# The last four row groups as one pair and two singles, with seven work tiles, five gate tiles, three cell tiles and two attention tiles

## The chip, the cores and the metric

The kernel runs on one core of a Trainium2 chip. The metric is the device time of one execution in microseconds (us), median of a few runs. A profiled execution has a span, which runs from its first to its last instruction, and a time of its own that lies a little above the span.

The engines go by the profile's names: PE is TensorE (PEld its weight loads), DVE is VectorE, ACT is ScalarE, POOL is GpSimd, and SP is SyncE, whose queue issues the transfers of the last phase.

## The reference

`x` has 128 batches of 64 nodes with 256 features, that is 8192 rows, and `adj` is a 64 x 64 matrix. Four graph layers follow one another, each as `x = layernorm(x + layer(x))`, all in float32:

- Layer 0 multiplies three times by `adj * adj` along the nodes and by a weight along the features (256 to 512 to 1024 to 256), with a ReLU after the first two.
- Layer 1 takes the eigenvectors `U` of a normalised Laplacian of `adj`, applies `U.T`, two small weights with a ReLU between, and `U`.
- Layer 2 applies `adj` and a weight twice, each with a ReLU, and then four LSTMs. For p = 1, 2, 3, 4, windows of p successive nodes are fed to LSTM p, and its last hidden state is written back at the last node of the window:

```python
for p in range(1, MAX_SKIP + 1):
    nw = Tv // p
    wins = h[:, :nw * p, :].reshape(Bv * nw, p, Hd)
    last = _lstm_last(Wih[p - 1], Whh[p - 1], bih[p - 1], bhh[p - 1], wins)
    idx = jnp.arange(nw) * p + (p - 1)
    h = h.at[:, idx, :].set(last.reshape(Bv, nw, Hd))
```

- Layer 3 is an attention within a batch: `h = x @ W + b_lin`, scores `h h^T` masked by `adj`, softmax, times `h`, plus `b`.

## The kernel before

The 8192 rows lie as 64 tiles of 128 rows, in 16 groups of 4 tiles, numbered 0 to 15. The first phase (to about 860 us of the span) does layer 0 for all groups and the eigenvectors in between. The second phase does layers 1, 2 and 3 for one group after another, and the change lies there alone.

In the second phase nothing is issued at once. Helpers (`Noted`, line 235; `products`, `turns`) write every operation into a `Plan` (line 104) with an assumed cost, the buffers that it reads and writes, and its predecessors. `Plan.run` (line 158) then picks the operations one by one, engine by engine, by the earliest time at which inputs, engine and a free buffer are there by its own clock, and emits them in that order. So the order of each engine's instructions is fixed when the program is built. As one helper emits everything, nearly all instructions of this phase carry line 156 in the profile, and one tells them apart by their tiles.

A **unit** is what `Plan.run` takes up at a time, with `UNITS = 3` units going side by side. Line 1554 makes the units: groups go in pairs up to `16 - SINGLE`, and the rest one by one.

```python
units = [(g, g + 1) for g in range(0, NT // 4 - SINGLE, 2)] + [(g,) for g in range(NT // 4 - SINGLE, NT // 4)]
plan.run([left_over] + [lambda u=u: unit(u) for u in units], UNITS)
```

`unit` (line 1518) does for each of its groups `layer1`, then `to_lstm` (the two products with `adj` and the LSTMs of p = 1, 2, 3), then the LSTM of p = 4, then `from_lstm` (the state transposed back, added to the rows, normalised) and `layer3`. A pair and a single group differ only in the LSTM of p = 4:

```python
if len(groups) == 2:
    four(hTs)
else:
    lstm(hTs[0], 4, 0, 16)
```

- `lstm` (line 1378) makes each gate of a step from four matmuls of 128 x 128 weights (two for the input, two for the hidden state) that stream 128 columns (16 windows of 8 batches). The first step has three gates and no hidden state. A gate goes from PSUM (tile `ps`) through a tanh on ACT into a tile `gates`; DVE then makes the cell `c` and the hidden state `hs`.
- `four` (line 1502) takes the first step the same way for each group. For the steps 1 to 3 it calls `halves` (line 1439), which treats the two groups and the two halves of the weights as a 2 x 2 block product and does it with seven products in place of eight. For that, DVE makes four differences or sums of the states (in a tile `w`), and seven more additions for each half `h` put the gates together. The sums of the weights (`sums`) are made once.

The last groups, `ENDING = (14, 15)`, do `layer3` in two parts of two tiles, and their row normalisations end on ACT (`norm`, line 1232, with `scalar`): statistics on DVE, four small operations on POOL (`rs`, `nm`), and then ACT applies them to `X`. After that SP stores the tile. In the other groups DVE applies them.

Buffers are slots of a tag: `w` (4 KB in each partition, `WIDE` of them; transposed rows, LSTM states, attention inputs), `gates` (4 KB, `GATES`), `c` (2 KB, `CELLS`), `hs` (`OUTS`), `att` (2 KB, `ATT`, cleared once by POOL), `v`, and the eight banks `ps`. A guard in `candidates` (line 168) lets a unit that is not the oldest take a slot only if enough stay free for the oldest (`MOST`, line 112: 4 of `w`, 2 of `gates`, 1 of `c` and of `att`).

When no unit is left to begin and at most `LASTS` groups have work left, the guard is dropped, and `rank` (line 163) lets PE take the group with the most operations left first.

Of the kernel before, what the change touches and what calls it, by code (L numbers as in the profile page):

```python
# [103 lines left out]
class Plan:  # L104
# [53 lines left out]
    def run(self, units, ways):  # L158
# [4 lines left out]
        def rank(op):  # L163
            if op.engine == "PE" and not todo and len(left) <= LASTS:
                return -left[op.group]
            return op.group or 99

        def candidates(guard):
            oldest = min([u for u in going if u] or [0])
            best = None  # L170
            for e, ops in able.items():
                first = []
                for op in ops:
                    t = max(self.free[e], op.ready)
                    for tile in op.tiles:
                        if tile.real is None and tile.slot is None:
                            s = self.slots[tile.tag]
                            t = max(t, min(s))

                            if (guard and op.unit != oldest and  # L180
                                    sum(x < 1e9 for x in s) <= self.MOST.get(tile.tag, 1) - held.get((oldest, tile.tag), 0)):
                                t = 1e9
                    if t < 1e9:
                        first.append((t, op))
                if first:
                    t0 = min(t for t, _ in first)
                    t, op = min((x for x in first if x[0] <= t0 + 0.02), key=lambda x: (rank(x[1]), x[1].rank))
                    if best is None or t < best[0]:
                        best = t, op
            return best  # L190

        while todo or going:
            while todo and len(going) < ways + (0 in going):
# [4 lines left out]
                for op in self.ops:  # L198
                    left[op.group] = left.get(op.group, 0) + 1
                    if not op.left:  # L200
                        able[op.engine].append(op)
            t, op = (candidates(True) if todo or len(left) > LASTS else None) or candidates(False)
            e = op.engine
# [535 lines left out]
EPS = 1e-5  # L739
UNITS = 3  # L740
ENDING = (14, 15)
WIDE = 6
GATES = 6
ATT = 3
CELLS = 4
OUTS = 4
LASTS = 3
SINGLE = 4

RING = 6  # L750

# [56 lines left out]
def kernel(  # L808
# [337 lines left out]
    att = []  # L1146
    for i in range(ATT):
        att.append(wb.tile([P, 4, P], F32, name=f"att{i}"))
# [3 lines left out]
    def place(tag, slot, shape):  # L1152
# [4 lines left out]
        if tag in ("w", "v", "gates", "c", "hs"):  # L1157
# [3 lines left out]
    plan = Plan({"PE": nc.tensor, "DVE": nc.vector, "ACT": nc.scalar, "POOL": nc.gpsimd, "SP": nc.sync}, place,  # L1161
                {"ps": 8, "w": WIDE, "v": 4, "gates": GATES, "c": CELLS, "hs": OUTS, "att": ATT, "mx": 4, "sm": 4, "st": 4, "mv": 4,
                 "rs": 4, "nm": 4})
# [354 lines left out]
    def unit(groups):  # L1518

        if groups[0] == 0:  # L1520
            add_weights(2, 30.0)
            add_weights(4, 60.0)
        xs, hTs = [], []
        for g in groups:
            plan.group = g + 1
            x = plan.tile("rows", [P, 4, D], rows_of(g % RING))
            xs.append(x)
            layer1(x)
            hTs.append(to_lstm(x))
        plan.group = groups[0] + 1  # L1530
# [4 lines that stand above are left out]
        for g, x, hT in zip(groups, xs, hTs):  # L1535
            plan.group = g + 1
            from_lstm(x, hT, g)
            if g in ENDING:
                layer3(x, g, 0, 2)
                layer3(x, g, 2, 2)  # L1540
            else:
                layer3(x, g, 0, 4)
            if g + RING < NT // 4:
                Q.dma_start(x, rest[g])
# [7 lines left out]
    with tc.manual_schedule(engines={mybir.EngineType.PE, mybir.EngineType.DVE, mybir.EngineType.Activation,  # L1552
                                     mybir.EngineType.Pool}):
        units = [(g, g + 1) for g in range(0, NT // 4 - SINGLE, 2)] + [(g,) for g in range(NT // 4 - SINGLE, NT // 4)]
        plan.run([left_over] + [lambda u=u: unit(u) for u in units], UNITS)
# [42 lines left out]
```

## Time and profile before

| | |
|---|---|
| median of 3 runs | 2471.87 us (2471.45 to 2472.79) |
| the profiled execution, its own time | 2474.36 us |
| its span | 2472.6 us |
| granted clock of PE, mean | 0.996 |
| busy in the span: PE / PEld / DVE / ACT / POOL | 99% / 87% / 65% / 43% / 6% |
| second phase, from about 860 us: PE / DVE busy | 1583 us / 963 us of 1612 us |
| transfers | 42.69 MB, most of it in the first slice |

The first block of the page gives each engine's busy time, the second the same in 40 equal slices of about 62 us, in tenths. A matmul in float32 appears as two records; a transpose appears as one. Matmuls are pipelined, so the duration of a record is longer than the distance to the next one; the distance is what a matmul costs when PE is full.

### The profile page before, as it was taken

The numbers are of one execution on the slowest core, as the hardware profiler recorded it, in microseconds if no ns is written. First come the engines' busy times: TensorE is split into PE (matmuls) and PEld (weight loads), VectorE is DVE, ScalarE is ACT, GpSimd is POOL, SyncE is SP. The second block draws the span as 40 slices with busy tenths as digits, with TensorE's granted clock in tenths as the row PEclk, the third lists the DMA queues.
The fourth block names the chain that finished last, engine by engine and source line by source line (L and its number), as shares of the span: only waits on it lengthen the run. The fifth ranks groups of instructions, "written<-read, shape, count | busy, mean of one in ns | idle before, by whom it ended". The sixth has DMA issues, their size and how long they took to land.

```text
span 2472.6 us, 40811 instructions
## 1 busy us (share of the span) xinstructions
PE 2438.2 (99%) x15500; PEld 2162.5 (87%) x15500; DVE 1618.9 (65%) x5676; ACT 1072.3 (43%) x2610; POOL 137.4 (6%) x316
## 2 busy tenths in 40 slices
PE   9999999999999999999999999999999999999997
PEld 7788888878887899989978999999998997988996
DVE  6888787778887274583674476476458468374336
ACT  2343343333333354444434444444444444445555
POOL 0000000000000010010010000000001001010002
PEclk9999999999999999999999999999999999999999
DMA  6000000000000110010000001001001000000000
GB/s 225 9 1 18 10 9 10 9 10 9 10 1 1 64 56 1 1 35 1 1 18 18 1 1 35 1 1 35 1 1 35 1 1 18 1 10 1 1 1 27
DMA packets 27973, 42.69 MB, mean 17 GB/s; under 512 B 2945, under 2 KB 22145, under 8 KB 27777
## 3 DMA queue, kind: packets, MB, share of 16 engines
q1 hardware_dynamic: 27424, 39.81, 4.6%
q8 instruction: 122, 2.00, 0.3%
q14 instruction: 75, 0.61, 0.1%
q10 hardware_dynamic: 352, 0.28, 0.0%
HBM read 26.45 MB, written 13.63 MB: 16 GB/s over the span
## 4 chain that ended last, share of the span: by engine, by line
PE 93%; DVE 5%; POOL 1%; DMA 1%; ACT 0%; issue 0%; SPq 0%; ACTq 0%; POOLq 0%; DVEq 0%
PE ps L156 61%; PE ps L940 31%; DVE X L156 1%; DVE D L52 1%; DVE st L156 1%; PE pc L296 1%; DMA XA<-in_x_dram 1%; DVE gates L156 0%; POOL rs L156 0%; DVE tw L52 0%; DVE w L156 0%; ACT gates L156 0%; DVE h L52 0%; DVE u L52 0%; DVE mv L156 0%
## 5 line engine op out<-in xcount | busy, mean ns | idle before, releaser
L156 PE MATMUL ps<-w,wih 128*128 128x168 f32 (+2 forms) x4144 | 753.7, 315 | 0.9 <-DVE gates L156 0.9
L156 PEld LDWEIGHTS ps<-w,wih 128*128 128x128 f32 x4144 | 647.6, 191 | 38.1 <-issue 6.9
L156 ACT ACTIVATE gates<-ps,cbi 128x168 f32<-128x168 f32 (+2 forms) x832 | 342.8, 418 | 368.5 <-PE ps L156 360.3
L156 PE MATMUL ps<-hs,whh 128*128 128x168 f32 (+1 forms) x1952 | 344.8, 291 | 0.0
L156 PEld LDWEIGHTS ps<-hs,whh 128*128 128x128 f32 x1952 | 289.2, 191 | 1.7 <-issue 1.4
L156 PE MATMUL ps<-w,sums 128*128 128x128 f32 x1776 | 237.1, 275 | 0.0
L156 DVE SCALAR_TENSOR_TENSOR gates<-gates 128x256 f32<-128x256 f32 (+2 forms) x220 | 84.0, 382 | 222.8 <-ACT gates L156 222.2
L940 PE MATMUL ps<-aw,h 128*128 128x256 f32 x1024 | 227.2, 379 | 0.0
L156 PEld LDWEIGHTS ps<-w,sums 128*128 128x128 f32 x1776 | 217.5, 192 | 0.6 <-issue 0.5
L940 PEld LDWEIGHTS ps<-aw,h 128*128 128x128 f32 x1024 | 192.9, 190 | 25.9 <-ACT h L949 0.5
L156 ACT ACTIVATE gates<-gates,cbi 128x256 f32<-128x256 f32 x272 | 116.4, 497 | 206.6 <-DVE gates L156 206.5
L949 ACT ACTIVATE h<-h 128x512 f32<-128x512 f32 x128 | 80.5, 630 | 196.6 <-DVE h L52 196.5
L156 DVE TENSOR_TENSOR gates<-gates,ps 128x256 f32<-128x256 f32 x340 | 128.7, 417 | 21.3 <-PE ps L156 15.9
L940 PE MATMUL ps<-ss,tw 128*128 128x256 f32 x512 | 117.9, 380 | 0.0
L940 PE MATMUL ps<-ss,aw 128*128 128x256 f32 x512 | 117.3, 379 | 0.0
L940 PE MATMUL ps<-m,aw 128*128 128x256 f32 x512 | 117.1, 380 | 0.0
L156 DVE SCALAR_TENSOR_TENSOR c<-gates,c 128x256 f32<-128x256 f32 (+2 forms) x156 | 57.2, 367 | 88.6 <-ACT gates L156 88.2
L940 PE MATMUL ps<-aw,m 128*128 128x512 f32 x256 | 114.8, 594 | 0.1
L940 PEld LDWEIGHTS ps<-ss,aw 128*128 128x128 f32 x512 | 96.6, 190 | 12.8
L940 PEld LDWEIGHTS ps<-ss,tw 128*128 128x128 f32 x512 | 96.3, 190 | 12.9 <-issue 0.2
L156 DVE TENSOR_TENSOR gates<-v,ps 128x256 f32<-128x256 f32 x136 | 55.5, 417 | 79.5 <-ACT v L156 47.7
L940 PEld LDWEIGHTS ps<-m,aw 128*128 128x128 f32 x512 | 95.6, 190 | 12.6 <-issue 0.5
(314 smaller groups left out, 3743.0 us busy)
## 6 DMA issues: line engine op xcount, KB each, us to landing
out_dram<-X SPq DMA_DIRECT2D x64, 128.0 KB, 1.7
rest<-XA SPq DMA_DIRECT2D x10, 512.0 KB, 2.6
X<-rest SPq DMA_DIRECT2D x10, 512.0 KB, 3.2
XA<-in_x_dram SPq DMA_DIRECT2D x18, 256.0 KB, 6.2
wih<-in_c_ih_dram SPq DMA_DIRECT2D x4, 1024.0 KB, 7.4
aw<-in_a_w_dram SPq DMA_DIRECT2D x3, 1024.0 KB, 10.8
X<-in_x_dram SPq DMA_DIRECT2D x12, 256.0 KB, 5.9
whh<-in_c_hh_dram SPq DMA_DIRECT2D x3, 1024.0 KB, 9.3
```

What stands on the lines that cost most here:

```text
L52: return getattr(self.engine, name)(out, *args, **kw)
L156: getattr(e, name)(*[real(x) for x in args], **{k: real(v) for k, v in kw.items()})
L296: PE.matmul(out, lhsT, rhs, start=True, stop=True)
L940: PE.matmul(out, lhsT, rhs, start=start, stop=stop)
L949: S.activation(dst, src, AF.Relu)
```

## The change

Six numbers at the head of the second phase are changed, and nothing else:

```diff
 ENDING = (14, 15)
-WIDE = 6
-GATES = 6
-ATT = 3
-CELLS = 4
+WIDE = 7
+GATES = 5
+ATT = 2
+CELLS = 3
 OUTS = 4
-LASTS = 3
-SINGLE = 4
+LASTS = 2
+SINGLE = 2
```

`SINGLE = 2` makes groups 12 and 13 a pair, so that seven pairs and two singles are left of six pairs and four singles. `LASTS = 2` applies the rule of the ending when two groups are left, not three. The four buffer counts give one tile of `w` (4 KB in a partition) for one of `gates` (4 KB), and free one of `c` and one of `att` (2 KB each). As all orders come from the plan, every engine's order in the second phase is a new one; the first phase keeps its order.

## The prediction

> **What bounds the kernel now.** I read the page's first two blocks, then tables of busy time by stretch, then the timeline of PE alone.
>
> ```profile
> span 2472.6 us, 40811 instructions
> PE 2438.2 (99%) x15500; PEld 2162.5 (87%) x15500; DVE 1618.9 (65%) x5676; ACT 1072.3 (43%) x2610; POOL 137.4 (6%) x316
> ```
>
> PE is the bound: 34.4 us of the span are without it. So a matmul less is worth its full price, and all else must come out of those 34.4 us. Where they lie is seen by stretch (columns: stretch, length, busy PE, PEld, DVE, ACT, POOL, then the clock granted to PE, DMA share, GB/s):
>
> ```profile
> 861.00:1250.00 389.00, 388.07 (x2800) 362.83 (x2799) 240.71 (x683) 184.33 (x450) 24.17 (x49) 1.00 0.05 20
> 1250.00:1320.00 70.00, 63.85 (x390) 50.40 (x389) 50.67 (x146) 29.35 (x59) 9.47 (x20) 0.95 0.09 31
> 1320.00:2030.00 710.00, 708.47 (x5167) 661.04 (x5166) 433.56 (x1274) 329.25 (x798) 35.55 (x72) 1.00 0.03 10
> 2030.00:2070.00 40.00, 36.36 (x273) 28.57 (x272) 32.59 (x94) 17.54 (x34) 5.85 (x12) 1.00 0.00 1
> 2070.00:2420.00 350.00, 349.63 (x2537) 330.50 (x2536) 168.47 (x504) 171.84 (x442) 12.36 (x24) 1.00 0.02 6
> 2420.00:2473.00 53.00, 36.87 (x286) 29.72 (x284) 36.74 (x125) 25.16 (x61) 15.07 (x40) 0.88 0.09 31
> ```
>
> PE idles 6.15 us at 1250 to 1320, 3.64 us at 2030 to 2070, 16.1 us in the tail from 2420, and 2.8 us in the other three together. In the two stretches in the middle DVE is 72% and 81% busy, against 60% around them; the finer table by 10 us has it at 9.4 to 9.9 of 10 at the worst places. The longest gap, on PE's timeline:
>
> ```profile
> 1302.32 1.29 PE L156 MATMUL ps<-adT,X 128*128 128x128 f32 x8 [3.64 <-DVE X L156]
> 1303.41 8.88 PE L156 MATMUL ps<-w,wih 128*128 128x256 f32 x33
> ```
>
> PE waited 3.64 us for DVE's normalised rows. After it, 33 records took 8.88 us; at the 0.2145 us of a full PE (two records of 256 columns 0.43 us apart near 2446) they would take 7.1. So the gap cost a further 1.8 us at a lower clock, and the two stretches cost 6.15 + 1.8 + 3.64 = 11.6 us.
>
> **What the Trainium skill says.** "TensorE: Matmul & The Clock Gate", section "What's actually happening", has the clock halved after an idle window of about 3.4 us, and restored after as much busy time. The trace agrees: the 3.64 us gap is followed by slow matmuls, while 2030 to 2070, whose longest gap is 2.05 us, stays at 1.00. "Perfetto Trace Analysis", section "Optimization Strategy", says to look for gaps on the bounding engine and what blocks it, and that a gap that repeats can mean too few buffers. Here the gaps do not repeat: two places hold most of them, behind a crowded DVE. I take that as a matter of order, which buffer counts decide only through the plan.
>
> **The change part by part.**
>
> *Groups 12 and 13 as a pair.* Two singles of p = 4 issue 2 x (3 gates x 2 halves x 2 + 3 steps x 4 x 2 x 4) = 2 x 108 = 216 matmuls of 128 columns. A pair issues 24 in its first step and 3 x 2 x 7 products x 4 = 168 after it: 192. So **24 fewer**, and the counts of the two built programs say the same (7976 and 7952 PE instructions, no other size touched). The price, from PE's timeline:
>
> ```profile
> 2405.26 0.61 PE L156 MATMUL ps<-hs,whh 128*128 128x128 f32 x4
> 2405.70 0.61 PE L156 MATMUL ps<-w,wih 128*128 128x128 f32 x4
> ...
> 2410.62 0.61 PE L156 MATMUL ps<-hs,whh 128*128 128x128 f32 x4
> ```
>
> From 2405.26 to 2410.62 there are 12 steps of two matmuls in 5.36 us, 0.2233 us each. 24 x 0.2233 = **5.4 us less**, all on the bound.
>
> *What it adds on DVE:* 42 additions of 256 columns (30 at 0.379, 12 at 0.408 us: 16.3), 24 differences of the states at 0.27 (6.6), 22 operations on `gates`, `c`, `hs` at 0.42 (9.3), less 44 of half the width at 0.29 (12.8): **+19.4 us**. ACT: 48 fewer tanh of one gate (0.352), 24 more of two (0.428), and small ones: -5.6 us. Both are hidden as long as DVE is not the last: DVE has about 60% in the phase. POOL clears one `att` less. SP's 142 transfers stay; none is moved past another that matters, as the rows of a group come in a whole unit ahead.
>
> *The order in the middle.* This is the unknown. The trace of before cannot show a new order, so I bound it: at best all 11.6 us of the two stretches go; at worst stalls of that kind grow (see rivals). To choose between, I laid DVE's instructions of the two built programs against PE's, in bins of 4 us of PE work, with durations from the trace, and carried DVE's surplus on. In the kernel before, the surplus is largest at 400 to 436 us of PE work (4.2 and 3.3 us, the place of the first stretch), at 1160 to 1192 (3.7, the second), and at 1012 (3.4, no gap of note). In the changed order no surplus is over 3.1 us, and only three are over 2.1; yet the densest 40 us still hold 40.1 us of DVE work, as before (40.4). So the crowding is spread rather than gone. I take half of the 11.6, rounded: **-5.5 us**. Fewer `gates`, `c` and `att` tiles I cost at nothing beyond this: waits for them show in no row of before, and the plan lays other groups' matmuls there.
>
> *The ending.* Take E as the end of the last LSTM matmul. Before, E is 2426.4 (2425.76 + 0.61), and 46.2 us follow, with 27.0 us of PE work in them (the third-last group's layer 3 is still to do): 19.3 us without PE. In the new order only the layer 3 of 14 and 15 is left, 19.1 us of PE work, and the transposes of both groups stand right behind E with nothing between. By durations of the trace: tanh 0.4, four copies on ACT (0.6 each) to E + 2.8; PE's transposes to 3.4; DVE's four sums (0.65) to 4.4, first statistics at 5.5; POOL 1.6 us for a normalisation, the next 1.67 later (2463.95 and 2465.62): 7.2, 8.9, 10.5, 12.2; ACT, which applies them between its copies, is through at 15.9; the last weight product follows at 18.7; 8.5 us of PE work and some 3.5 us of waits for exponentials put PE's end at 30.7; DVE 2.4, POOL two normalisations, ACT 1.1 and the store (2.6, from 2470.0 to the end) give E + 39.7. That is 20.5 us without PE, **+1.2 us**, give or take 3: what is late is POOL's chain and then ACT, which nothing covers any more.
>
> *Steps with two groups alone.* For 100 us before E only 14 and 15 remain. A step's first use of `hs` has at least 1.34 us of PE work between it and the last gate; before, the same places had 1.14 and 1.34, inside stretches with PE at 100%. Cost 0.
>
> Sum: -5.4 - 5.5 + 1.2 = **-9.7 us**. The execution that gave the durations took 2474.36 us, 1.8 more than its span and 2.5 more than the median of the runs; I take the difference from the median: 2471.87 - 9.7 = **2462.2 us**.
>
> **The rivals.**
>
> *Stalls stay as they are.* The crowded stretches only move. For it: the densest 40 us are as dense. Against: the surplus is smaller. Then -5.4 + 1.2 = -4.2: 2467.7 us.
>
> *Stalls go altogether,* and the ending costs nothing more: -5.4 - 11.6 = -17: 2454.9 us. Against: 40.1 us of DVE work in 40.
>
> *DVE becomes the bound in three places, slower than before.* The new order has dense stretches at 388, 1180 and 1376 us of PE work (40.1, 39.0 and 33.8 us of DVE in 40), and one gate and one cell tile less to fill PE with other groups. Were each to stall as 1250 to 1320 did, clock included (7.95 us), that is 23.9 against 11.6: +12.3 - 5.4 + 1.2 = +8.1: 2480 us. It decides once stalls in the middle exceed 20.7 us. Against: before, equally dense stretches (39.1 us at 592) cost 0.3 us.
>
> That the change does not do what it says is excluded by the counts.
>
> **How the numbers follow.** A measurement of this kernel can tell about 0.2%, 4.9 us, from no change. Stalls halved or better, with the full-gain rival: 0.73, all faster. Stalls as before: 0.18, nearly all within 0.2%, though its ending's 3 us reach across. DVE-bound: 0.09, two thirds slower. So faster 0.74, same 0.19, slower 0.07. The range runs from the full gain with 1 us more (2454) to stalls slightly grown (2472).
>
> **What would show it.** Right: 24 matmuls fewer at the same 0.223 us; PE's idle between 861 us and the tail down from 12.6 to about 7; no gap over 3 us in the middle, the clock at 1.00 throughout; about 40 us from the last LSTM matmul to the end. Wrong: a gap of 3.6 us or more behind `DVE X`, PE waits for `gates` or `c`, or over 43 us after E.

## The result, and the profile after

The changed kernel takes 2458.3 us (median of five runs, 2458.1 to 2458.67) against 2471.56 us for the kernel before beside it (2470.68 to 2472.79): a ratio of 0.9942, 95% interval 0.9932 to 0.9953, that is 13.3 us less. The forecast was 2462.2 us, 9.7 us less, with a range of 2454 to 2472. Its direction and its range held; the sum behind it did not, since two of its terms were wrong, by about 10 and by 4 us, and in opposite directions.

The profiled execution of after took 2458.3 us, as its median. That of before took 2474.36 us, 2.8 us more than its median, so the two profiles lie 16.1 us apart where the medians lie 13.3 apart.

The span and the engines' busy time from the head of the page of after, to be laid beside those of before:

```profile
span 2456.4 us, 40740 instructions
PE 2431.3 (99%) x15452; PEld 2155.8 (88%) x15452; DVE 1636.9 (67%) x5720; ACT 1069.3 (44%) x2586; POOL 138.5 (6%) x315
```

PE has 48 records fewer, which are the 24 float32 matmuls of two records each. DVE is 18 us busier (19.4 were forecast), and PE's idle time has gone from 34.4 to 25.1 us. Where it went is seen by stretch (columns as before: stretch, length, busy PE, PEld, DVE, ACT, POOL, granted clock, DMA share, GB/s):

```profile
861.00:1250.00 389.00, 388.99 (x2817) 364.80 (x2817) 243.00 (x684) 186.75 (x457) 22.67 (x45) 1.00 0.05 19
1250.00:1320.00 70.00, 69.54 (x475) 58.72 (x474) 54.95 (x160) 33.72 (x73) 9.96 (x20) 1.00 0.09 31
1320.00:2030.00 710.00, 708.98 (x5131) 657.51 (x5131) 433.08 (x1266) 330.60 (x787) 38.67 (x76) 1.00 0.03 10
2030.00:2070.00 40.00, 40.00 (x291) 33.32 (x290) 35.62 (x109) 20.13 (x45) 5.69 (x12) 1.00 0.01 1
2070.00:2405.00 335.00, 334.28 (x2447) 314.03 (x2446) 188.02 (x560) 158.78 (x397) 15.64 (x32) 1.00 0.02 7
2405.00:2457.00 52.00, 33.93 (x238) 27.21 (x236) 25.30 (x90) 24.51 (x61) 11.34 (x32) 0.84 0.07 21
```

The two places where PE stood before are full: 69.54 of 70 us and 40.00 of 40, although DVE has about as much to do there for each busy us of PE as it had (0.79 us in the first place before and after, 0.90 and 0.89 in the second). From 861 us to the ending PE idles 2.2 us in all, where it idled 12.6. The ending went the other way: 18.1 us idle in 52, and a clock of 0.84. PE's own timeline shows the ending (columns: start, duration, group, and in brackets the idle time before it with what ended it); 2412.71 is the end of the last LSTM matmul, called E as in the prediction:

```profile
2412.10 0.61 PE L156 MATMUL ps<-hs,whh 128*128 128x128 f32 x4
...
2413.71 2.27 PE L156 MATMUL ps<-ident,w 128*128 128x128 f32 x15 [0.66 <-ACT w L156]
2420.27 1.18 PE L156 MATMUL ps<-ident,X 128*128 128x128 f32 x4 [4.29 <-ACT X L156]
2422.20 1.18 PE L156 MATMUL ps<-ident,X 128*128 128x128 f32 x4 [0.75 <-ACT X L156]
2423.16 1.92 PE L156 MATMUL ps<-w,dw 128*128 128x256 f32 x4
...
2443.56 0.56 PE L156 MATMUL ps<-ident,att 128*128 128x128 f32 x2 [1.90 <-ACT att L156]
2443.95 3.56 PE L156 MATMUL ps<-w,v 128*128 128x256 f32 x8
```

PE waits 4.29 us for the first rows that ACT has normalised, and is slow behind that: four transposes take 1.18 us where before took 0.60, four product records 1.92 where it took 1.03. The last eight `w,v` records, after a second wait of 1.90 us, take 3.56 us where before took 1.99. E to the end is 43.7 us. The same groups at full clock, in before:

```profile
2433.82 0.60 PE L156 MATMUL ps<-ident,X 128*128 128x128 f32 x4
2434.25 1.03 PE L156 MATMUL ps<-w,dw 128*128 128x256 f32 x4
...
2452.53 1.99 PE L156 MATMUL ps<-w,v 128*128 128x256 f32 x8
```

### The profile page after: what moved, and what is told of

It is laid out like the page before. It is cut to its first block, busy times and chain, and to the rows that moved or that the text cites. A ratio compares the mean times of both kernels' runs of the same rounds, so it can differ in the third digit from the quotient of the medians.

```text
span 2456.4 us, 40740 instructions
## 1 busy us (share of the span) xinstructions
PE 2431.3 (99%) x15452; PEld 2155.8 (88%) x15452; DVE 1636.9 (67%) x5720; ACT 1069.3 (44%) x2586; POOL 138.5 (6%) x315
## 4 chain that ended last, share of the span: by engine, by line
PE 96%; DVE 3%; DMA 1%; issue 0%; POOL 0%; ACT 0%; SPq 0%; ACTq 0%; POOLq 0%; DVEq 0%
PE ps L156 63%; PE ps L940 31%; DVE D L52 1%; PE pc L296 1%; DMA XA<-in_x_dram 1%; DVE tw L52 0%; DVE X L156 0%; POOL rs L156 0%; DVE h L52 0%; DVE u L52 0%; DVE st L156 0%; ACT X L156 0%; DVE w L52 0%; DVE ss L52 0%; PE pa L296 0%
## 5 line engine op out<-in xcount | busy, mean ns | idle before, releaser
L156 PE MATMUL ps<-w,wih 128*128 128x128 f32 (+2 forms) x4024 | 738.9, 316 | 0.9 <-DVE gates L156 0.9
L156 PEld LDWEIGHTS ps<-w,wih 128*128 128x128 f32 x4024 | 632.4, 191 | 36.3 <-issue 6.2
L156 ACT ACTIVATE gates<-ps,cbi 128x168 f32<-128x168 f32 (+2 forms) x784 | 325.5, 421 | 346.8 <-PE ps L156 339.7
L156 PE MATMUL ps<-hs,whh 128*128 128x168 f32 (+1 forms) x1808 | 325.6, 293 | 0.0
L156 PEld LDWEIGHTS ps<-hs,whh 128*128 128x128 f32 x1808 | 271.2, 191 | 0.8 <-issue 0.5
L156 PE MATMUL ps<-w,sums 128*128 128x128 f32 x1944 | 259.7, 275 | 0.0
L156 PEld LDWEIGHTS ps<-w,sums 128*128 128x128 f32 x1944 | 238.6, 192 | 2.1 <-issue 1.7
L156 ACT ACTIVATE gates<-gates,cbi 128x256 f32<-128x256 f32 x296 | 126.4, 497 | 207.4 <-DVE gates L156 207.4
L156 DVE TENSOR_TENSOR gates<-gates,ps 128x256 f32<-128x256 f32 x370 | 140.3, 417 | 18.6 <-PE ps L156 12.8
L156 POOL TENSOR_SCALAR rs<-mv 128x2 f32<-128x2 f32 x96 | 25.5, 265 | 1460.4 <-DVE mv L156 1443.0
```

The lines of the kernel that those rows point to most:

```text
L156: getattr(e, name)(*[real(x) for x in args], **{k: real(v) for k, v in kw.items()})
```

## The experiments

All edits are to the kernel before unless the line says otherwise. The programs show in advance how few parts the change has: with six `w` tiles, 5 `gates`, 3 `c` and 2 `att` give the order of the kernel before, with its 6, 4 and 3, on every engine (POOL clears one `att` less); and after with 6 `gates` has the order of after. So these three counts change no order; they make room. What changes the order is the seventh `w` tile on one side, and the pair with `LASTS = 2` on the other.

### The pair alone, the seventh tile alone

```diff
-LASTS = 3
-SINGLE = 4
+LASTS = 2
+SINGLE = 2
```

> Only the pair and the rule of the ending are changed (SINGLE 2, LASTS 2), the buffers stay at 6, 6, 3, 4. Theory A (the gain in the middle comes with the seventh w tile): the first crowded stretch at 1250 to 1320 us stays with its 6 us of idle PE and its slow clock, as the order is that of before up to there; 5.4 us of matmuls go and the ending costs 5 us more, the second stretch may change with the new neighbours: 2466 to 2472 us. Theory B (the pair itself makes the gain): within 3 us of the changed kernel, 2456 to 2461 us.

Measured: 2479.74 us, a ratio of 1.003 (1.0018 to 1.0041), **7.4 us slower**. Both theories expected a gain and both missed.

```diff
-WIDE = 6
-GATES = 6
-ATT = 3
-CELLS = 4
+WIDE = 7
+GATES = 5
+ATT = 2
+CELLS = 3
```

> Only the buffers are changed (7, 5, 2, 3), six pairs and four singles stay. Theory A: PE's idle from 861 us to the tail falls from 12.6 us to about 2 and no slow clock is left there, with the old ending and the 24 matmuls still done: 12 to 14 us less than before, 2457 to 2460 us, about the time of the whole change. Theory B: 2469 to 2473 us.

Measured: 2457.01 us, 0.9939 (0.9925 to 0.9952), **15.3 us faster**, as much as the whole change. So theory A holds in its main point: the tile brings the gain, and the 24 matmuls are not needed for it. Two stretches of the pair alone, then the same two of the buffers alone:

```profile
1250.00:1320.00 70.00, 63.84 (x397) 51.52 (x397) 51.59 (x148) 30.96 (x62) 9.44 (x20) 0.98 0.09 31
...
2070.00:2405.00 335.00, 327.75 (x2314) 305.53 (x2313) 186.45 (x551) 157.98 (x385) 15.79 (x32) 0.99 0.02 7
```

```profile
1250.00:1320.00 70.00, 69.55 (x475) 58.73 (x474) 54.82 (x159) 33.70 (x73) 9.94 (x20) 1.00 0.09 31
...
2070.00:2405.00 335.00, 334.94 (x2471) 318.19 (x2470) 160.03 (x481) 163.85 (x423) 11.17 (x23) 1.00 0.02 6
```

With six tiles the pair keeps the stall at 1250 us (6.16 us idle) and adds 7.25 us of idle time in the last stretch, where two groups are to fill PE alone. With seven tiles the stall is gone whether there is a pair or not, although DVE is 54.8 us busy in those 70 us against 50.67 in the kernel before, 0.79 us for each busy us of PE in both. The amount of DVE's work there thus doesn't account for the stall by itself. All that PE waits for between 861 and 2400 us in the kernel with the buffers alone (columns: us, times, longest) is:

```profile
PE ps L156 <- DVE w L156: 0.9, 3, 0.4
PE ps L156 <- DVE gates L156: 0.9, 1, 0.9
```

The first two lines of the same list for the pair alone:

```profile
PE ps L156 <- DVE w L156: 5.2, 4, 3.2
PE ps L156 <- DVE X L156: 4.8, 3, 3.6
```

### Is it the tile, or the luck of another order?

Each change of a count gives a new order, and a new order can be better by chance. So the order was disturbed without any change of buffers: the plan takes any operation that could begin within 0.02 us of the first by its rank; here within 0.05.

```diff
-... if x[0] <= t0 + 0.02), key=...
+... if x[0] <= t0 + 0.05), key=...
```

> The kernel before with another order alone: the plan takes operations as equally early within 0.05 and not 0.02 us of its clock, everything else as it was. Theory C (the stalls of before are an accident of its order, and any fresh order loses them): 2457 to 2462 us. Theory D (with six w tiles the crowding comes back in any order, and the surplus of DVE work over PE work tells how much; here its largest values are 6.8 and 4.8 us against 4.2 and 3.7): 2469 to 2477 us.

Measured: 2492.38 us, 1.0077 (1.0065 to 1.009), **20 us slower**. Theory D is right in direction and too small in size. The stall at 1250 us is gone (69.88 busy of 70), but a new place holds 14.9 us of idle time, with the clock down:

```profile
1430.00:1490.00 60.00, 45.15 (x301) 35.53 (x301) 41.95 (x124) 18.38 (x39) 6.97 (x16) 0.86 0.06 20
```

The same disturbance with seven tiles (5 `gates`, 3 `c`, 2 `att`):

> The buffers-only kernel (seven w tiles) with the same disturbance of the order that cost the kernel before 20 us (operations taken as equally early within 0.05 us). Theory A (seven tiles leave slack, so that an order matters little): 2456 to 2463 us. Theory C (orders are accidents of this size with any buffers): 2466 us or more.

Measured: 2462.75 us, 0.9961 (0.9947 to 0.9976), in theory A's range: the disturbance costs 5.7 us with seven tiles and 20 with six. PE idles 6.9 us from 861 to 2405 (1537.13 busy of 1544), against 22.8 with six. The seventh tile therefore helps with both rules tried, by 15.3 and by 29.6 us, so one lucky order is an unlikely reading. But an order by itself can be worth some 6 us even with seven.

```diff
-WIDE = 6
+WIDE = 5
```

> The kernel before with five w tiles instead of six, nothing else. Theory A (each w tile less leaves PE with less to do while DVE is crowded): more and longer gaps in the middle; by the surplus of DVE work, up to 8.3 us in five places, some 25 to 50 us above before: 2495 to 2520 us. Theory C (the order is an accident, the count of w tiles is not the reason): anywhere within 10 us of the kernel before.

Measured: 2542.6 us, 1.0285 (1.027 to 1.03), **70 us slower**: theory A has the direction, but expected 50 us at most. And eight tiles (5 `gates`, 3 `c`, 2 `att`):

> Six pairs and four singles with eight w tiles, 5 gates, 2 att, 3 c: the buffers-only kernel with one w tile more. Theory A, saturated: with seven PE was idle for about 2 us in the middle, so there is nothing left to win: 2455 to 2459 us. Theory G (more w tiles also help the ending, where PE idles for 17 us): 2450 to 2454 us.

Measured: 2463.25 us, 0.9962 (0.9947 to 0.9977), 6.2 us worse than seven; both theories missed. The whole second phase up to the ending, for five, then for eight:

```profile
861.00:2405.00 1544.00, 1486.49 (x10404) 1358.65 (x10403) 907.55 (x2595) 689.54 (x1646) 85.83 (x177) 0.98 0.04 12
```

```profile
861.00:2405.00 1544.00, 1536.89 (x11105) 1426.99 (x11104) 921.16 (x2684) 726.32 (x1768) 87.78 (x177) 1.00 0.04 12
```

PE idles 57.5 us with five tiles, 12.6 in the profile with six, 2.1 with seven, 7.1 with eight. The way from five to seven is large and goes one way. Eight differs from seven by about what a disturbance of the order costs.

Why a tile does this is argued, not shown. The guard lets a younger unit take a `w` tile only if four stay for the oldest, and the plan can be counted as it is laid: it holds back 53 operations for want of a `w` tile with five, 33 with six, 15 with seven and 11 with eight, and none at any count for want of `gates`, `c` or `att`. That goes with the times up to seven. Counted the same way, it holds back more operations for want of a PSUM bank (135, 252, 222 and 168), which does not go with them. And five to eight also differ in everything else that an order decides. Six tiles with three in place of four kept for the oldest would set the guard apart from the tile; it wasn't tried.

### The ending

In after PE waits 4.29 us behind E with nothing to do and is slow thereafter. To separate the slow clock from the wait, 32 products whose results nothing uses were added for that gap. They stand behind the normalisation of group 15 in the program and need only its last state (edit to after, in `from_lstm`):

```diff
+        if g == 15:
+            p = ps4()
+            for i in range(32):
+                run(p[:, :P], [(hb[:, i % 2, 384:], ident)])
```

> The changed kernel with 32 matmuls more (128 columns, result unused, 7.1 us of PE work) behind the last group's state, which the plan lays in the two gaps before the rows are normalised. Theory E (the gap of 4.3 us costs a second time, as PE runs at a low clock after it): the clock of the stretch after it is 1.00 and not 0.67, the transposes and products there take 2 to 3 us less, and the time falls by 1 to 3 us. Theory F (the ending is bound by the normalisations on POOL and ACT, and PE's clock is free there): same within 0.5 us, or up to 2 us longer where the filler is in the way.

Measured: 2454.84 us, 0.9926 (0.9913 to 0.9938), **3.5 us faster** than after in its own five runs, 2.6 us faster than after in a repeat. More work for the bounding engine made the kernel faster, and the clock behind the gap is up, as theory E had it. First after's slice of 10 us, then that of the kernel with the added products, with its timeline:

```profile
2420.00:2430.00 10.00, 8.98 (x50) 7.01 (x51) 0.93 (x5) 7.44 (x19) 3.82 (x11) 0.67 0.00 0
```

```profile
2420.00:2430.00 10.00, 10.00 (x93) 8.85 (x92) 2.39 (x11) 5.95 (x17) 2.70 (x8) 1.00 0.01 2
```

```profile
2414.20 7.74 PE L156 MATMUL ps<-ident,w 128*128 128x128 f32 x68
2421.77 1.47 PE L156 MATMUL ps<-ident,X 128*128 128x128 f32 x12
2423.08 1.10 PE L156 MATMUL ps<-w,dw 128*128 128x256 f32 x4
```

Behind E (2414.36 here) PE now has no gap until it takes the normalised rows at 2421.77. The clock is 1.00 instead of 0.67, four product records take 1.10 us and not 1.92, and E to the end is 39.6 us, not 43.7.

How much of the gain is the clock's stays open, for the added operations also changed the plan's order. Eight transposes and four of the added records now lie ahead of E, which comes 1.65 us later, and one of the two groups is ahead of the other: ACT is through with four of the eight tiles of rows at E + 1.2, where in after it begins with the first at E + 6.9. First ACT with the added products, then in after:

```profile
2414.93 0.59 ACT L156 ACTIVATE X<-X,nm,rs 128x256 f32<-128x256 f32 x1
```

```profile
2419.61 1.09 ACT L156 ACTIVATE X<-X,nm,rs 128x256 f32<-128x256 f32 x2 [4.23 <-POOL nm L156]
```

So what POOL and ACT have to normalise behind E is about halved as well. Nor is the clock up to the end: after a wait of 2.77 us the last product records are slow here too (four in 2.08 us, at 2441.69). A version with the products added and the order of after was not run.

The repeat of after, unchanged, beside the later kernels:

> The changed kernel itself, unchanged, beside the three above on one chip, so that they are compared under the same conditions: 2457.5 to 2459 us by every theory. Its profile shows a second time whether the gap of 4.3 us and the clock near 0.67 in the ending are there in each execution.

Measured: 2457.4 us, 0.9938 (0.9925 to 0.995), with a gap of 4.28 us at the same place and a clock of 0.74 in the same slice. After and the buffers alone (2457.0) are equal. With seven tiles the pair as the change places it brings nothing, though it saves 24 matmuls. Three kernels change the rule of the ending and the pair one at a time. With the guard, and the usual order of groups on PE, kept to the very end (edit to after):

```diff
-LASTS = 2
+LASTS = 0
```

> The changed kernel with LASTS 0: at the end PE takes the earlier group first, so that group 14 is through before 15. Theory H (the ending loses its time because 14 and 15 finish together and nothing covers their normalisation): 14's normalisation lies under 15's last LSTM steps, only 9.6 us of PE work instead of 19.1 follow the last LSTM matmul, and the ending idles for 5 us less: 2452 to 2455 us. Theory I (one group alone then waits at each of its last steps, with 0 to 1.3 us of work between the last gate and the next step): 2458 to 2464 us.

Measured: 2470.46 us, 0.9993 (0.9984 to 1.0002), 13.1 us worse than the repeat of after and worse than both theories. The last two groups then go one behind the other, and PE stands already before the ending, for `w`:

```profile
2280.00:2400.00 120.00, 111.44 (x778) 103.04 (x778) 55.43 (x168) 59.26 (x153) 6.63 (x18) 0.97 0.02 5
```

```profile
2445.98 1.18 PE L156 MATMUL ps<-ident,X 128*128 128x128 f32 x4 [4.33 <-ACT X L156]
```

The long gap of the ending stays too. With `LASTS` as before (edit to after):

```diff
-LASTS = 2
+LASTS = 3
```

> The changed kernel with LASTS 3, as before the change: pair 12 and 13, then 14 and 15; 20.4 us of PE work follow the last LSTM matmul, 1.3 more than in the changed kernel. Theory J: hardly more cover, so within 2 us of the changed kernel: 2456 to 2460 us. Theory L': the rule alone made the ending worse: 2451 to 2454 us.

Measured: 2460.02 us, 0.9948 (0.9934 to 0.9961), 2.6 us worse than the repeat, at the upper end of theory J's range. The gap is longer:

```profile
2422.51 1.18 PE L156 MATMUL ps<-ident,X 128*128 128x128 f32 x4 [5.39 <-ACT X L156]
```

Without the pair and with `LASTS = 2` (edit to the buffers alone):

```diff
-LASTS = 3
+LASTS = 2
```

> The buffers-only kernel with LASTS 2: no pair, all matmuls as before, but the rule of the ending waits for two groups left, and 19.1 us of PE work follow the last LSTM matmul. Theory J: this ending costs what the changed kernel's costs, without the matmuls saved: 5 to 7 us above the buffers-only kernel, 2462 to 2464 us. Theory L (LASTS is without effect on the time, the pair is what spoils the ending): 2456 to 2458 us.

Measured: 2468.45 us, 0.9983 (0.9976 to 0.999), 11.4 us worse than the buffers alone, and worse than both theories; theory J expected 5 to 7. The ending gets a gap of 3.10 us, and a stall of 3.2 us appears ahead of it, at 2300 to 2350 us, where the buffers alone fill 50.00 of 50:

```profile
2300.00:2350.00 50.00, 46.76 (x325) 45.45 (x324) 24.18 (x72) 23.60 (x61) 0.00 (x0) 0.93 0.00 1
```

As far as these kernels show, what covers the wait behind E is a third group's layer 3, still to do at that point; it is there in the kernel before and with the buffers alone. Without the pair, `LASTS = 2` takes it away; with the pair ahead of two singles the long gap is there under either value. Last, a version that has both, the matmuls saved and a single group ahead of the pair (edit to the buffers alone):

```diff
-        units = [(g, g + 1) for g in range(0, NT // 4 - SINGLE, 2)] + [(g,) for g in range(NT // 4 - SINGLE, NT // 4)]
+        units = [(g, g + 1) for g in range(0, 12, 2)] + [(12,), (13, 14), (15,)]
```

> Seven w tiles as in the change (7, 5, 2, 3), LASTS 3, and seven pairs, but the last pair is 13 and 14, with 12 and 15 single around it: the same 24 matmuls fewer as in the change, while three groups run at the end, and 27.4 us of PE work instead of 19.1 follow the last LSTM matmul. Theory J (the pair's 5.4 us are real, and the changed kernel gives them back only because two groups alone end together): the ending as in the buffers-only kernel, 5 us less than that one's 2457.0: 2450 to 2453 us, no PE gap over 2 us in the ending and its clock at 1.00 until PE runs out. Theory K (the pair itself costs its gain, by DVE work on the way): 2456 to 2459 us.

Measured: **2453.18 us**, 0.9921 (0.9908 to 0.9933), the fastest of all, 0.2 us above theory J's range. It is 3.8 us faster than the buffers alone, of the 5.4 that 24 matmuls cost. No gap in its ending is over 1.1 us, yet the clock is not at 1.00 as expected, but 0.89 and 0.94 between 2410 and 2430 us:

```profile
2415.81 1.48 PE L156 MATMUL ps<-ident,X 128*128 128x128 f32 x8 [1.06 <-DVE X L156]
2418.10 5.20 PE L156 MATMUL ps<-w,dw 128*128 128x512 f32 x8 [0.81 <-DVE w L156]
```

## Why the prediction was right or wrong

The forecast came out within 4 us by luck: two mis-sized terms went against each other. The terms, as changes from the kernel before in the profiled executions ("middle" is the time from the start of the second phase to E less PE's work in it; "ending" is E to the end less PE's work at full clock):

| | 24 matmuls | middle | ending | sum | spans differ by |
|---|---|---|---|---|---|
| predicted | -5.4 | -5.5 | +1.2 | -9.7 | |
| after | -5.4 | -15.5 | +5.3 | -15.6 | -16.2 |
| the pair alone | -5.4 | +5.9 | +3.8 | +4.3 | +4.1 |
| the buffers alone | 0 | -15.3 | -1.7 | -17.0 | -17.7 |

- **The matmuls: right.** 48 records fewer, as forecast. As a gain the price of 5.4 us was not reached in any kernel: the version with the pair inside gains 3.8 us over the buffers alone, and in after the ending takes it all back.
- **The middle: the step "I take half of the 11.6" failed.** What stood in its place is more than all of it: 10.4 us of idle time and 3.5 us of slow clock are gone, 1.6 us I cannot place, and 2.8 us of the slower profiled execution of before may lie in any of these. Two things were wrong in it. The cause: I took the stalls for a crowded DVE and read the density of DVE's work, but in after DVE has about as much to do there for each busy us of PE, and PE is full; the stalls go with the seventh `w` tile. And the size: 1.7 us of slow clock was overlooked, behind two short waits that the last section shows. The measure of DVE's surplus, carried on into some of the expectations, put the disturbed order and five tiles on the slow side and seven on the fast one, but with far too small sizes: at most 5 us for a disturbance that cost 20. Of the rivals, "stalls go altogether" was right for the middle.
- **The seventh tile was never priced as a cause.** The prediction named fewer tiles of three kinds and costed them at nothing. That fits: with six `w` tiles the order is the same with and without them. The added tile it treated as a part of a new order.
- **The ending: +1.2 predicted, +5.3 measured.** The chain itself was right nearly step by step: PE's transposes through at E + 3.3 (3.4 predicted), first statistics at E + 5.2 (5.5), POOL's first normalisation at E + 6.9 (7.2), ACT's last copies at E + 17.2 (15.9), and the last 8.9 us from PE's end to the end (9.0). What failed is the step from there: PE's work was taken at full clock (8.5 us up to PE's end among it), although the chain itself left PE idle for over 3.4 us. Behind the two gaps PE's records cost 4.3 us more than at full clock: 2 x 0.58 for transposes (1.18 against 0.60), 0.89 for four product records, 0.68 for the next eight, and 1.57 for the last `w,v`. That is about the whole difference from the forecast, 4.1 us. For the gap of 4.29 us, and so for 2.7 of the 4.3 us, the prediction had the matching rule in its own text, from the Trainium skill ("TensorE: Matmul & The Clock Gate", section "What's actually happening"), used it for the middle, and did not use it here. The other 1.6 us follow a wait of 1.90 us, which that rule does not reach; the last section comes to it.
- **"Steps with two groups alone: cost 0" held for after** (PE idles 0.7 us from 2070 to 2405 us), but not in the kernels beside it: with six tiles the same stretch idles 7.25 us, with seven tiles, `LASTS = 2` and no pair 3.6 us, and with `LASTS = 0` 8.6 us in 120. It rests on the order.
- **The rival that ended slower** (new stalls of 20.7 us or more) describes what six tiles do in a disturbed order, 22.8 us idle. It didn't happen in after.
- **The signs to watch.** "No gap over 3 us in the middle, the clock at 1.00 throughout" came true. "Over 43 us after E" was given as a sign of a wrong step, and it was one: 43.7.

## What to carry to other kernels

Where a planner lays the order, vary the count of each buffer alone before taking a stall for a busy engine: here one more work tile was worth 15 us, and 24 matmuls fewer without it made the kernel 7 us slower. A gap on the bounding engine can be paid twice, as the wait and as slow work behind it (in after 4.3 us of it), so it is worth having independent work behind the last dependent step; one group left over for that (2453.2 us) did better than either edit of the change. And one disturbance of the order moved this kernel by about 6 us with seven tiles and by 20 with six, so one order more or less proves little.

## What the hardware showed that was not expected

In several places the clock falls without any single gap over 3.4 us. In the kernel before, PE's last product ahead of 1266 us ends at 1265.66; then it waits 0.80 us, transposes for 1.6 us, and waits 0.81 us, and the next eight records of 512 columns take 5.40 us. Four of them took 1.88 us at 1280 us, so some 3.7 us would be full speed. On PE's timeline, then in a stretch of 2 us:

```profile
1266.46 1.57 PE L156 MATMUL ps<-ident,X 128*128 128x128 f32 x8 [0.80 <-DVE X L156]
1268.85 5.40 PE L156 MATMUL ps<-w,dw 128*128 128x512 f32 x8 [0.81 <-DVE w L156]
```

```profile
1270.00:1272.00 2.00, 2.00 (x3) 0.69 (x3) 1.97 (x7) 0.00 (x0) 0.89 (x3) 0.50 0.00 0
```

So the clock is halved there, after 3.2 us with no work on PE but transposes. The version with the pair inside shows the same: 1.06 us of waiting, eight transposes, 0.81 us, then the same products in 5.20 us. So does after ahead of its last `w,v` records: no product from 2440.79 to 2443.95, also 3.2 us, with waits of 0.43 and 1.90 us in it. And the pair alone, whose gap behind E is 3.10 us, has the same slow records behind it (four transposes in 1.18 us, four product records in 1.91). The Trainium skill has a sentence that fits ("TensorE: Matmul & The Clock Gate", section "Part 4: PE-mode transpose"): a transpose doesn't count as busy for the clock in the way a product does. A transpose would then be idle time in that count, and in after the stretch without a product lasts from 2412.71 to 2423.16. The runs don't prove it, and it can't be the whole rule. Behind E the kernel before and the one with the buffers alone run the same transposes with the same waits (0.24, 0.85, 0.25 and 0.26 us in one; 0.23, 0.85, 0.25 and 0.26 in the other), and no product for over 4 us. Yet the eight product records that follow take 2.81 us in before, with the clock at 0.50 from 2430 to 2432 us, and 1.89 us at a clock of 1.00 with the buffers alone. First before:

```profile
2431.17 2.81 PE L156 MATMUL ps<-w,dw 128*128 128x256 f32 x8
```

```profile
2414.47 1.89 PE L156 MATMUL ps<-w,dw 128*128 128x256 f32 x8
```

With the seven transposes ahead of them (1.76 us against 1.11) that is 1.6 us, most of the -1.7 us in the ending of the buffers alone in the table. What decides between the two is not in the order of the operations and stays open; small differences of the ending's cost between two kernels can come from it. None of the kernels sets transposes against products in such a place with all else equal.
